# The last head pair's softmax sums on 64 rows a head, in a fused attention and convolution kernel on one NeuronCore

## The chip, the cores and the metric

The kernel runs on 1 core of one Trainium2 chip, in one launch. The metric is the device time of that launch in microseconds (us), the median of 3 runs.

## The reference

Two residual layers are applied to `x` of shape (8, 768, 32, 32), all in float32. Each normalises its input over 32 groups of channels first (`_gn`).

```
x = x + _L0_conv_ref(_gn(x), W_qkv, W_proj, b_proj)    # layer 0
x = x + _L1_conv_ref(_gn(x), conv_w, conv_b)           # layer 1

# layer 0, per image: 1024 tokens, 12 heads of 64 channels
q, k, v = (x_flat @ W_qkv.T) split in three
var_v, var_k = variance of v and of k over the 64 channels of a head (ddof=1)
attn = softmax(var_v @ var_k^T * 64**-0.5)             # 1024 x 1024 a head, of rank 1 before the softmax
out  = (attn @ v) @ W_proj.T + b_proj

# layer 1: a 1x1 convolution over the 768 channels and 28 correlations of the
# normalised feature with itself, shifted along four lines through a 7x7 window
out = einsum('bchw,oc->bohw', concat([feature, corr]), conv_w) + conv_b
```

`q` is not used. What matters here is `attn @ v`, its division by the softmax's sums, and the projection that reads the result.

## The kernel before

The work goes image by image (0 to 7). For each image there are, in the order of TensorE's program: products for keys and values (`KeysValues`), attention of the 12 heads as six pairs `hp` = 0 to 5 (`Pair`, `Attention`), and the projection (`project`). The convolution of the image before (`Conv`) and the second half of the keys' and values' products are strewn among the attention steps to keep TensorE busy. The big products follow a scheme of seven products for a 2 x 2 block; a product is named by its group and its number, (g, p), and `LOWS` gives the projection's order: (0,1), (2,1), (1,1), (0,5), (1,5), (2,5), then (0,6), (1,6) and so on, and at the end (2,6), (2,3), (2,7), (2,2), (2,4).

**The order of instructions.** Each engine runs its instructions in the order in which the Python program issues them; semaphores between engines are added automatically. That order is made by a planner, the class `Clock`: `clock.now` is a planned time, `pass_time(us)` moves it on after a unit of TensorE's work was issued, and `later.after(us, job)` has a job issue its instructions when the planned time reaches it. `clock.dve` is the planned end of VectorE's queue, and `after_dve(us, job)` counts from there. A planned time only decides what is issued before what; on the chip an instruction waits for its data.

**Evictions.** `Banks` hands out PSUM banks to the products. `Banks.close` plans the eviction of a product (a VectorE addition) for 0.1 us after the product's planned end, which is just after the next product was issued. In `project` group 2 uses the two banks of a tile `own`, the bank pair of attention's results, as its "home" slots.

**A pair.** For each of 8 blocks of keys, ScalarE computes the exponentials `ex` (L764) and TensorE multiplies them with the values into `av` (L789). The softmax's sums come in one of two ways. For some pairs ScalarE computes exponentials a second time with the accumulated sum (`denominators`, L774), and `invert` and `spread` invert and transpose the sums and write them to DRAM. For the pairs in `SUMMED` (0, 3, 4, 5 in image 0, and 3, 4, 5 in the others) VectorE adds up the exponentials in two tiles `acc`, one for each head, and a product with ones sums over the partitions. For all pairs but the last, `load_inverses` then loads the inverses from DRAM into `rd` and sets `rd_at`, the planned time of their arrival; `try_finish` plans `finish`, the multiply `v<-v,rd` on VectorE, for then. `rdpool` has one buffer, so a pair's load is issued only after the pair before has finished.

**The last pair** (`hp` = 5) ends in `sum_up_last`. Four matmuls with 32 columns of ones (`ones_products`, L820) put the sums of two heads and two halves of the tokens on four groups of 32 partitions of one bank `den`. Two reciprocals write the inverses to `acc[1]`, and eight DMAs of 64 KB (L886), four on SP's queue and four on ACT's, copy them to the 64 partitions of each head in `acc[0]`. The multiply then is `v<-v,acc`.

**The projection.** `project` issues `t1o` (`TokenSums.first`) and the first six products, which need pairs 0 to 2 alone. Before the seventh it waits, in planned time, for the last pair; `TokenSums.second` (tiles `t2o`) is issued ahead of the first product (from the third on) that is issued after the last pair's multiply. The seventh product (0,6) is the first to read `t2o`.

## Time and profile before

| | |
|---|---|
| median of 3 runs | 2656.31 us (2655.44 to 2657.39) |
| profiled execution | 2660.47 us, span 2658.7 us |
| TensorE matmul (PE) busy | 2605.5 us, 98% |
| VectorE (DVE) busy | 1576.7 us, 59% |
| ScalarE (ACT) busy | 1367.2 us, 51% |
| GpSimd (POOL) busy | 414.9 us, 16% |
| DMA | 452.39 MB, mean 170 GB/s |
| mean granted TensorE clock | 0.994 |

A view's row names the line of the kernel, the engine, the operation and the tiles it writes and reads (`out<-in`); a timeline's row begins with its start and its length in us, merges like instructions (`x12`), and ends with the idle time before it and what ended that. A float32 matmul shows as two records, so a product of six matmuls shows as `x12`. L347 is the helper that issues products, L164 the wrapper of all VectorE instructions, so tiles tell them apart. SPq is SP's queue, which issues most DMAs in order.

### The profile page before, as it was taken

The numbers are of one execution on the slowest core, as the hardware profiler recorded it, in microseconds if no ns is written. First come the engines' busy times: TensorE is split into PE (matmuls) and PEld (weight loads), VectorE is DVE, ScalarE is ACT, GpSimd is POOL, SyncE is SP. The second block draws the span as 40 slices with busy tenths as digits, with TensorE's granted clock in tenths as the row PEclk, the third lists the DMA queues.
The fourth block names the chain that finished last, engine by engine and source line by source line (L and its number), as shares of the span: only waits on it lengthen the run. The fifth ranks groups of instructions, "written<-read, shape, count | busy, mean of one in ns | idle before, by whom it ended". The sixth has DMA issues, their size and how long they took to land.

```text
span 2658.7 us, 40713 instructions
## 1 busy us (share of the span) xinstructions
PE 2605.5 (98%) x14814; PEld 1361.2 (51%) x14814; DVE 1576.7 (59%) x4094; ACT 1367.2 (51%) x1841; POOL 414.9 (16%) x444
## 2 busy tenths in 40 slices
PE   9999999999999999999999989999999999999999
PEld 5654455334764247642476424764247643575333
DVE  5868634865348653486535765357753576535764
ACT  1497089701797017970189601896018960189500
POOL 4320130003300043000430003300033001320000
PEclk9999999999999999999999999999999999999999
DMA  7875467365563645636556355563554646545333
GB/s 284 293 243 170 131 196 208 96 201 159 174 200 102 209 151 170 198 113 199 157 169 197 124 184 154 171 207 115 190 169 154 200 126 197 165 137 168 120 98 104
DMA packets 326926, 452.39 MB, mean 170 GB/s; under 512 B 60738, under 2 KB 246450, under 8 KB 326726
## 3 DMA queue, kind: packets, MB, share of 16 engines
q1 hardware_dynamic: 323958, 444.93, 52.9%
q10 hardware_dynamic: 2768, 4.85, 0.5%
q8 instruction: 118, 1.93, 0.3%
q14 instruction: 82, 0.67, 0.1%
HBM read 376.70 MB, written 64.40 MB: 166 GB/s over the span
## 4 chain that ended last, share of the span: by engine, by line
PE 92%; DVE 3%; DMA 3%; SPq 1%; issue 1%; ACT 0%; POOL 0%; DVEq 0%; ACTq 0%; POOLq 0%
PE x L347 33%; PE av L789 24%; PE y L347 16%; PE z L347 9%; PE own L347 4%; PE gr L1131 3%; DMA acc<-acc 1%; PE den L820 1%; DMA wt<-tsp 1%; DVE xn L164 1%; DVE f L164 1%; PE y L1038 1%; DVE acc L164 0%; PE z L1038 0%; SPq L886 0%
## 5 line engine op out<-in xcount | busy, mean ns | idle before, releaser
L764 ACT ACTIVATE ex<-bc,nk 128x1024 f32<-128x1024 f32 x768 | 826.8, 1137 | 409.3 <-DMA bc<-vdr 172.7
L789 PE MATMUL av<-ex,v 128*64 128x512 f32 x3072 | 697.5, 594 | 2.7 <-ACT ex L764 2.6
L789 PEld LDWEIGHTS av<-ex,v 128*64 128x64 f32 x3072 | 333.2, 137 | 318.1 <-issue 182.7
L774 ACT ACTIVATE junk<-bk,vm 128x1024 bf16<-128x1024 f32 x368 | 420.5, 1143 | 27.7 <-DMA bk<-kdr 18.0
L164 DVE TENSOR_TENSOR acc<-acc,ex 128x1024 f32<-128x1024 f32 x300 | 345.1, 1212 | 0.0
L226 ACT COPY kp<-x 128x384 f32<-128x384 f32 x28 | 13.4, 478 | 572.5 <-PE x L347 563.8
L347 PE MATMUL y<-kv,s 128*64 128x384 f32 x1488 | 267.6, 487 | 0.0
L347 PE MATMUL x<-kv,xn 128*64 128x384 f32 x1512 | 262.6, 486 | 1.1 <-issue 1.1
L347 PE MATMUL x<-kv,s 128*64 128x384 f32 x1488 | 256.7, 486 | 0.0
L347 PEld LDWEIGHTS x<-kv,xn 128*64 128x64 f32 x1512 | 143.1, 137 | 100.0 <-issue 83.9
L347 PEld LDWEIGHTS x<-kv,s 128*64 128x64 f32 x1488 | 144.3, 137 | 91.5 <-issue 72.3
L347 PEld LDWEIGHTS y<-kv,s 128*64 128x64 f32 x1488 | 140.9, 137 | 89.8 <-issue 74.0
L520 POOL TENSOR_TENSOR rstda<-vea,neghalf 128x1 f32<-128x1 f32 x8 | 4.8, 597 | 1005.1 <-DVE vea L164 1005.1
L1116 POOL TENSOR_TENSOR turn<-f,ones 128x384 f32<-128x384 f32 x112 | 111.0, 1012 | 241.1 <-PE gr L1131 154.6
L347 PE MATMUL z<-kv,xn 128*64 128x384 f32 x768 | 134.7, 486 | 0.0
L347 PE MATMUL x<-f,wt 128*64 128x512 f32 x504 | 119.0, 593 | 0.0
L626 POOL TENSOR_TENSOR s<-xn 128x384 f32<-128x384 f32 x64 | 67.7, 1068 | 311.3 <-PE x L347 190.7
L164 DVE TENSOR_TENSOR v<-y,v 128x128 f32<-128x128 f32 x180 | 41.0, 282 | 125.7 <-PE y L347 125.7
L164 DVE TENSOR_TENSOR v<-v,rd 128x1024 f32<-128x1024 f32 x40 | 48.7, 1218 | 101.4 <-DMA rd<-di 79.8
L164 DVE BATCH_NORM_STATS2 vbn<-v 128x6 f32<-128x64 f32 x720 | 101.6, 210 | 0.0
L347 PEld LDWEIGHTS z<-kv,xn 128*64 128x64 f32 x768 | 76.7, 137 | 45.9 <-issue 37.3
L1131 PEld LDWEIGHTS gr<-f,turn 128*64 128x64 f32 x1344 | 89.4, 136 | 11.3 <-issue 1.5
(200 smaller groups left out, 3093.0 us busy)
## 6 DMA issues: line engine op xcount, KB each, us to landing
kv<-kvs SPq DMA_DIRECT2D x124, 576.0 KB
kv<-in_wkv_dram SPq DMA_DIRECT2D x95, 576.0 KB
bc<-vdr SPq DMA_DIRECT2D x96, 512.0 KB
f<-in_x_dram SPq DMA_DIRECT2D x48, 512.0 KB
bk<-kdr SPq DMA_DIRECT2D x46, 512.0 KB
x1d<-f SPq DMA_DIRECT2D x42, 512.0 KB
xn<-x1d SPq DMA_DIRECT2D x42, 512.0 KB
out_dram<-xn SPq DMA_DIRECT2D x82, 256.0 KB
```

The source lines that it names most:

```text
L164: return getattr(self.engine, name)(*args, **kw)
L226: nc.scalar.copy(to, at)
L347: nc.tensor.matmul(out[at], lhsT=lhsT[:, at], rhs=rhs, start=start, stop=stop, **kw)
L520: nc.gpsimd.tensor_tensor(self.rstd, ve, neghalf[:, 0:1], ALU.pow)
L626: nc.gpsimd.tensor_tensor(self.sums[g][:, 0], a[g][2], a[g][3], ALU.add)
L764: nc.scalar.activation(ex, self.bc[e], AF.Exp, scale=self.kv.nk[self.half][:, h, t : t + 1])
L774: nc.scalar.activation(junk, self.bk[e], AF.Exp, scale=self.kv.m2[self.half][:, h, t : t + 1], accum_out=self.sums[:, e, t : t + 1],)
L789: nc.tensor.matmul(self.av[e * HD : (e + 1) * HD, hf, :], lhsT=self.vt[:, t, e, :], rhs=exs[e][:, hf * HF : (hf + 1) * HF], start=t == 0, ...
L820: nc.tensor.matmul(den[at * 32 : (at + 1) * 32, :], lhsT=ones[:, 0:32], rhs=self.acc[e][:, hf * HF : (hf + 1) * HF], start=True, stop=True,)
L1038: nc.tensor.matmul(t, lhsT=wcorr_sb[at, i, :], rhs=cs[at, tokens, :], start=False, stop=True, skip_group_check=True)
L1116: nc.gpsimd.tensor_tensor(to[:, :, side], half, windows(ones, ones.ap[0], (0, J), (HW, 4), (1, HW)), ALU.mult)
L1131: nc.tensor.matmul(ps[side * HD : (side + 1) * HD, :n].rearrange("p (y x) -> p y x", x=WIDE), lhsT=block[:, j, side, :], rhs=image[:, 4 * ...
```

## The change

1. `Banks.close`: evictions from the home slots (the two `own` banks) are planned 0.2 us earlier, so 0.1 us before the planned end of their product instead of 0.1 us after it.
2. `denominators`: in image 1, pair 2, the inversion is planned 3.0 instead of 0.5 us after the last sums.
3. `load_inverses`: for pairs 0 to 2 of every image, `rd_at` is 14 us after the load's issue; before, this held for pair 2 of image 1 alone, and all others had 8 us.
4. `sum_up_last`: four matmuls with 64 columns of ones put the sums of each head on its 64 partitions, in two banks, one for each half of the tokens. Four reciprocals of 128 x 256 write the inverses straight to `acc[0]`. The DMAs are gone. In images 1 to 7 the first reciprocal is planned 1.2 us after the products, and each other one 1.5 us after VectorE's planned queue has ended; in image 0 without these gaps.

```
         def close(self, slot, t, us, taken):
             job = self.due[slot] = lambda: taken(t)
-            clock.after(us + 0.1, lambda: self.due.get(slot) is job and self.finish(slot))
+            early = 0.2 if slot[0] == "home" else 0.0
+            clock.after(us + 0.1 - early, lambda: self.due.get(slot) is job and self.finish(slot))
...
                 self.bk_free = True
-                later.after(max(0.0, clock.act - clock.now) + 0.5, self.invert)
+                more = 3.0 if (self.b, self.hp) == (1, 2) else 0.5
+                later.after(max(0.0, clock.act - clock.now) + more, self.invert)
...
-            self.rd_at = clock.now + (14.0 if (self.b, self.hp) == (1, HP // 2 - 1) else 8.0)
+            self.rd_at = clock.now + (14.0 if self.hp < HP // 2 else 8.0)
             self.try_finish()
 
         def sum_up_last(self):
 
-            den = other([P, HF], f"den{self.b}_{self.hp}")
-            self.ones_products(den)
-            self.rd, rc = self.acc[0], self.acc[1][:, 0:HF]
-            q = HF // 2
+            dens = []
+            for hf in range(2):
+                at = slice(hf * HF, (hf + 1) * HF)
+                den = other([P, HF], f"den{self.b}_{self.hp}_{hf}")
+                for e in range(2):
+                    nc.tensor.matmul(
+                        den[e * HD : (e + 1) * HD, :], lhsT=ones, rhs=self.acc[e][:, at], start=True, stop=True
+                    )
+                dens.append(den)
+            self.rd = self.acc[0]
 
             def invert(n):
-                vector.reciprocal(rc[:, n * q : (n + 1) * q], den[:, n * q : (n + 1) * q])
-                later.after_dve(0.5, spread if n else lambda: invert(1))
-
-            def spread():
-                for at in range(4):
-                    e, hf = divmod(at, 2)
-                    to = self.rd[e * HD : (e + 1) * HD, hf * HF : (hf + 1) * HF]
-                    rows = rc[at * 32 : (at + 1) * 32, :]
-                    for half in range(2):
-                        (nc.scalar if e else nc.sync).dma_start(out=to[half * 32 : (half + 1) * 32, :], in_=rows)
-                self.rd_at = clock.now + 5.0
-                self.try_finish()
-
-            later.after(1.7 if self.b else 1.0, lambda: invert(0))
+                q = HF // 2
+                vector.reciprocal(self.rd[:, n * q : (n + 1) * q], dens[n // 2][:, n % 2 * q : (n % 2 + 1) * q])
+                if n < 3:
+                    later.after_dve(1.5 if self.b else 0.0, lambda: invert(n + 1))
+                else:
+                    self.rd_at = clock.dve
+                    self.try_finish()
+
+            later.after(1.2 if self.b else 0.0, lambda: invert(0))
```

## The prediction

> **What bounds the kernel now.** I read the page first, then the chain, then TensorE's waits, then the timelines around each wait. The page's busy times and its chain:

> ```profile
> PE 2605.5 (98%) x14814; PEld 1361.2 (51%) x14814; DVE 1576.7 (59%) x4094; ACT 1367.2 (51%) x1841; POOL 414.9 (16%) x444
> ...
> PE 92%; DVE 3%; DMA 3%; SPq 1%; issue 1%; ACT 0%; POOL 0%; DVEq 0%; ACTq 0%; POOLq 0%
> ```

> TensorE is never short of work for long, so a change counts only as far as it alters TensorE's work or its waits. TensorE's waits (total us, times, longest):

> ```profile
> PE x L347 <- DVE t2o L164: 18.9, 6, 4.8
> PE own L347 <- DVE f L164: 15.6, 14, 1.7
> PE x L347 <- DVE xn L164: 4.8, 1, 4.8
> ...
> PE av L789 <- ACT ex L764: 2.6, 2, 1.3
> ```

> The first and third are the place of `sum_up_last`: once per image, in images 1 to 7. The second is the `own` banks at the end of `project`. Timelines of image 2, TensorE, VectorE, SP queue:

> ```profile
> 874.15 1.07 PE L820 MATMUL den<-acc,ones 128*32 128x512 f32 x8
> ...
> 888.08 2.74 PE L347 MATMUL own<-t1o,wt 128*64 128x512 f32 x12
> 894.56 7.93 PE L347 MATMUL x<-t2o,wt 128*64 128x512 f32 x24 [3.74 <-DVE t2o L164]
> ```

> ```profile
> 876.24 1.75 DVE L164 RECIPROCAL acc<-den 128x256 f32<-128x256 f32 x1
> ...
> 879.76 1.75 DVE L164 RECIPROCAL acc<-den 128x256 f32<-128x256 f32 x1
> ...
> 892.68 1.23 DVE L164 TENSOR_TENSOR v<-v,acc 128x1024 f32<-128x1024 f32 x1 [3.63 <-DMA acc<-acc]
> 893.82 1.89 DVE L164 TENSOR_TENSOR t2o<-v,t1o 128x512 f32<-128x512 f32 x3
> 895.62 0.74 DVE L164 SCALAR_TENSOR_TENSOR f<-own,bproj_sb,f 128x512 f32<-128x512 f32 x1
> ```

> ```profile
> 880.56 5.67 SPq L334 DMA_DIRECT2D wt<-tsp  x3
> ...
> 887.16 2.49 SPq L886 DMA_DIRECT2D acc<-acc  x4
> ```

> The inverses are ready at 881.5, but SP's four copies stand behind weight loads that wait for TensorE to free their buffers, and go out at 887.16. The multiply (892.68), `t2o` and the seventh product follow from that. And the stall costs more than its 3.74 us: 24 matmuls last 5.15 elsewhere and 7.93 here, each at half the pace for the first product. The same half pace follows all six stalls of 3.02 to 4.82 us (images 1 to 6) and none of those up to 1.71.

> The end of `project` in image 2:

> ```profile
> 925.74 2.74 PE L347 MATMUL own<-v,wt 128*64 128x512 f32 x12
> 929.34 2.79 PE L347 MATMUL own<-v,wt 128*64 128x512 f32 x12 [0.86 <-DVE f L164]
> 931.96 2.75 PE L347 MATMUL z<-v,wt 128*64 128x512 f32 x12
> 936.41 2.80 PE L347 MATMUL own<-t4o,wt 128*64 128x512 f32 x12 [1.71 <-DVE f L164]
> ```

> ```profile
> 928.53 0.75 DVE L164 SCALAR_TENSOR_TENSOR f<-own,bproj_sb,f 128x512 f32<-128x512 f32 x1 [3.01 <-PE own L347]
> ```

> The eviction at 928.53 belongs to product (2,6), over at 925.9, but ends its wait only with (2,3), which writes the other bank: the two banks are one tile, and the kernel orders work on it as one.

> **The change, part by part.** Times are against the profiled execution (2660.47 us, span 2658.7 and 1.8 around it); it lies 4.2 above the median of the runs, 2656.31, and I carry the difference over to the median. About 0.2% (5.3 us) can be told from no change.

> *Sums on 64 rows.* Four matmuls of 32 columns take 1.00 (874.15 to the next product, 875.15); four of 64 columns are an attention step, 1.72 (6.87 per 32 records, four steps). So TensorE has 0.72 more per image. Sixteen more reciprocals of 1.75 are 28 us of VectorE, in project, where it waits for products anyway. Gone are 64 DMAs of 64 KB, with 2.5 us of issue on each of SP and ACT per image; nothing on ACT waits there.

> *The new order, images 2 to 6.* The planner's clock gives it (it counts 1.74 a reciprocal, 0.68 an eviction, 2.58 a product). With the product (0,1) issued at 0, the others follow every 2.58, the sum is issued at −1.70, the reciprocals at −0.50, 3.04, 8.86 and 12.10, the multiply at 15.33, and with the 0.2 us of `early` the eviction of (2,5) at 15.38. `t2o` comes with the seventh product, (0,6), at 15.48. Before, that eviction stood at 15.58, behind `t2o` (895.62 against 893.82). VectorE's queue is then: reciprocal, t1o, two evictions, (0,1), reciprocal, (2,1), (1,1), reciprocal, (0,5), reciprocal, (1,5), multiply, (2,5), t2o. With row durations the fourth reciprocal ends 14.7 after the sums' start, (1,5) has been evicted at 15.5 and the multiply is over at 16.7, before (2,5) ends at 17.35: the inverses no longer hold anything. But `t2o` now stands behind the eviction of (2,5): (2,5) starts at 1.72 + 5 × 2.575 = 14.6, ends 2.75 later, then 0.05, eviction 0.66, and 0.74 from t2o's start to the product: 18.8. Unheld it would be 17.2, so 1.6 of idle remains, less than any stall that halved the pace. Before, the same distance was 20.41, 20.05, 21.43, 20.34 and 19.69: 101.9 − 94.0 = 7.9 gained. The half pace after it (two products took 7.77, 6.90, 8.20, 6.90, 6.90 against 5.15) gives 10.9. Together **−18.8**.

> *Image 1.* The sum is issued 11 us ahead of project, so all four reciprocals and the multiply fit: the multiply starts at 550.7 instead of 552.31 and, what matters, no longer stands before the last evictions of the convolution. Product (1,1), which waited for these until 556.66 (gap 4.82), starts at 552.4: −4.3, and −2.6 of half pace (5.17 for a product of 2.58). **−6.9**.

> *Image 7.* The same 18.8 against 17.01 now (gap 0.34, full pace): **+1.8**.

> *Image 0.* Here VectorE also has the statistics of the next image's keys, and the planner puts the multiply at 289.90, after the copy of the value rows, the eviction of (2,5) and six small scalings. (2,5) ends at 291.45; then copy 0.25 (with its transpose 0.3), eviction 0.66, scalings 0.9, multiply 1.14, 0.74: the seventh product at 295.5 instead of 290.57. +5.0, and since 4 us of idle is more than the 3.02 that halved the pace, 1.75 to 3.05 more (I take 2.2): **+7.2**.

> *Evictions of `own` ahead of the next product.* Now (2,3) must wait for (2,6)'s eviction and (2,7) for (2,3)'s. One such turn costs 929.34 − 925.74 − 2.58 = 1.0 to 1.2 (319.16 to 322.92 in image 0: 1.18); in place of one turn per image and, in images 2 to 6, 1.87 before (2,4) (0.4 in image 1) there are two turns and nothing before (2,4), whose eviction has (2,2) to hide in. Before 8 × 1.18 + 5 × 1.87 + 0.4 = 19.2, after 16 × 1.18 = 18.9: **−0.3**. If each also finds VectorE in a 0.76 us scaling of the next image, +9; if the other bank did not count, −19.

> *The inversion of pair 2 of image 1, 2.5 us later.* VectorE waited 8.34 for it at 465.18, ahead of accumulations that free exponentials; TensorE's gap there is 1.25. I take **−1.2** (bounds 0 and −1.5).

> *Multiplies of pairs 0 to 2, 6 us later.* VectorE idles 79.8 us before 15 of them, up to 11.4, yet TensorE's waits in attention are the two of 1.3 above: cover enough, so 0. If the 23 moved multiplies of 1.22 each met an eviction on the path, +28; the row with 11.4 and no gap is the nearest.

> Sum: −18.8 − 6.9 + 1.8 + 7.2 − 0.3 − 1.2 = −18.2, so **2638**.

> [...]

> **The rivals.**

> *Nothing holds t2o* (the eviction is issued after it, or image 0's chain is shorter): 1.6 less in images 2 to 7 and 7 less in image 0: 2638 − 9.6 − 7.2 = 2621. For it: image 0 shows no stall now. Against: the 0.1 us between 15.38 and 15.48. 15%.

> *The multiply slips* (the slower side). Its place is the seventh product of images 2 to 7: planned at 15.33, with 0.15 to spare. If a shift in attention makes it later than 15.48, or a reciprocal waits, the multiply runs behind (2,5)'s eviction: 1.14 more, 2.7 idle, and the pace halves again in six images. At 2.2 each that is +20, 2658; at two windows of half pace (3.4 each, as image 4 nearly shows with 3.05) +27, and 1.2 more in image 0: 2666. Slower from 2.8 us of half pace on. 15%, half of it beyond 2661.6.

> *Image 0's stall keeps the pace*: 2636. Against: all six stalls over 3 us lost it. [...] 5%.

> *The later due times do nothing*, as their multiplies still meet their DMA: that is the term 0, the time stays 2638.

> **How the numbers follow.** Forecast 60%, its own range 2630 to 2648 by the bounds of the half pace, the own banks and pair 2; 2621 15%, 2636 5%, the slip 15%, and 5% for a reordered attention anywhere up to 2670. The range 2619 to 2659 leaves out the far half of the slip and the tails. Faster by over 0.2% (under 2651): 0.60 + 0.15 + 0.05 + 0.02 = 0.82. Slower: 0.07 + 0.02 = 0.09. The same: 0.09.

> **What would show it.** Right: no wait on `DMA acc<-acc`; in images 2 to 7 an eviction of `own` just before `t2o`, gaps near 1.4 to 1.6 before the first product of `t2o` and 5.15 for the next two; four reciprocals per image between the evictions; in image 0 a gap near 4 before the same product; two gaps of 0.86 in `own`, before (2,3) and (2,7), none before (2,4). Wrong: the multiply behind that eviction, half pace in images 2 to 7, or new gaps inside attention.

## The result and the profile after

The changed kernel takes 2645.19 us (median of 6 runs, 2642.72 to 2650.47), the kernel before 2656.43 in the same series (6 runs, 2654.74 to 2659.37). The ratio is 0.9958, with a 95% interval of 0.9946 to 0.9971: faster by 0.4%. Forecast were 2638 us and a range of 2619 to 2659.

The two profiled executions lie further apart than the medians: 2660.47 before, 4.0 above its median, and 2642.72 after, 2.5 under its own. So the traces differ by 17.75 us and the medians by 11.2. The terms below are read from the traces and sum to the first. Two executions that took 4268.76 us (`e5_image0_copied`) and 14237.98 us (the kernel before) are left out of the figures below.

The page after, busy times and chain:

```profile
PE 2598.2 (98%) x14814; PEld 1329.4 (50%) x14814; DVE 1608.2 (61%) x4110; ACT 1367.7 (52%) x1841; POOL 416.9 (16%) x444
...
PE 95%; DVE 2%; DMA 1%; ACT 0%; issue 0%; SPq 0%; POOL 0%; DVEq 0%; POOLq 0%; ACTq 0%
```

VectorE is busy 31.5 us longer (1576.7 before; sixteen more reciprocals), yet its share of the chain falls from 3% to 2%. That of DMA falls from 3% to 1%. TensorE's waits after:

```profile
PE own L347 <- DVE f L164: 14.9, 16, 2.6
PE x L347 <- DVE t2o L164: 13.1, 7, 3.6
PE av L791 <- ACT ex L765: 2.2, 2, 1.3
PE den L822 <- DVE acc L164: 2.0, 1, 2.0
```

The seventh product still waits for `t2o`, now in seven images: 3.6 in image 0 and 1.45 to 1.81 in images 2 to 7. A new wait of 2.0 before the sums of a pair (`den`) has come. Image 2 after, TensorE and then VectorE:

```profile
876.52 1.94 PE L878 MATMUL den<-acc,ones 128*64 128x512 f32 x8
...
891.16 2.75 PE L347 MATMUL own<-t1o,wt 128*64 128x512 f32 x12
895.37 5.37 PE L347 MATMUL x<-t2o,wt 128*64 128x512 f32 x24 [1.46 <-DVE t2o L164]
```

```profile
877.67 1.76 DVE L164 RECIPROCAL acc<-den 128x256 f32<-128x256 f32 x1 [0.22 <-PE den L878]
...
883.01 1.75 DVE L164 RECIPROCAL acc<-den 128x256 f32<-128x256 f32 x1
...
886.90 1.75 DVE L164 RECIPROCAL acc<-den 128x256 f32<-128x256 f32 x1
...
889.47 1.75 DVE L164 RECIPROCAL acc<-den 128x256 f32<-128x256 f32 x1
...
892.05 1.21 DVE L164 TENSOR_TENSOR v<-v,acc 128x1024 f32<-128x1024 f32 x1
893.97 0.75 DVE L164 SCALAR_TENSOR_TENSOR f<-own,bproj_sb,f 128x512 f32<-128x512 f32 x1 [0.71 <-PE own L347]
894.64 1.88 DVE L164 TENSOR_TENSOR t2o<-v,t1o 128x512 f32<-128x512 f32 x3
```

The multiply waits for nothing any more and is over at 893.26. VectorE then idles 0.71 us for the product (2,5), because the eviction at 893.97 has been issued ahead of `t2o`. The next two products take 5.37 and not 7.93: the half pace is gone.

### The profile page after: what moved, and what is told of

It is laid out like the page before. It is cut to its first block, busy times and chain, and to the rows that moved or that the text cites. A ratio compares the mean times of both kernels' runs of the same rounds, so it can differ in the third digit from the quotient of the medians.

```text
span 2641.0 us, 40631 instructions
## 1 busy us (share of the span) xinstructions
PE 2598.2 (98%) x14814; PEld 1329.4 (50%) x14814; DVE 1608.2 (61%) x4110; ACT 1367.7 (52%) x1841; POOL 416.9 (16%) x444
## 3 DMA queue, kind: packets, MB, share of 16 engines
q10 hardware_dynamic: 1232, 2.75, 0.3%
## 4 chain that ended last, share of the span: by engine, by line
PE 95%; DVE 2%; DMA 1%; ACT 0%; issue 0%; SPq 0%; POOL 0%; DVEq 0%; POOLq 0%; ACTq 0%
PE x L347 34%; PE av L791 25%; PE y L347 17%; PE z L347 9%; PE own L347 5%; PE gr L1134 3%; DVE f L164 1%; PE den L822 1%; PE den L878 1%; PE y L1041 1%; PE z L1041 1%; DMA f<-in_x_dram 0%; ACT ex L765 0%; DMA bc<-vdr 0%; DMA xn<-in_x_dram 0%
## 5 line engine op out<-in xcount | busy, mean ns | idle before, releaser
L791 PEld LDWEIGHTS av<-ex,v 128*64 128x64 f32 x3072 | 324.6, 137 | 329.9 <-issue 206.6
L164 DVE TENSOR_TENSOR acc<-acc,ex 128x1024 f32<-128x1024 f32 x300 | 345.1, 1212 | 0.0
L347 PE MATMUL y<-kv,s 128*64 128x384 f32 x1488 | 266.8, 487 | 0.0
L347 PE MATMUL x<-kv,xn 128*64 128x384 f32 x1512 | 262.3, 486 | 1.1 <-issue 1.1
L347 PE MATMUL x<-kv,s 128*64 128x384 f32 x1488 | 256.6, 486 | 0.0
L347 PEld LDWEIGHTS x<-kv,xn 128*64 128x64 f32 x1512 | 137.9, 137 | 106.9 <-issue 91.2
L347 PEld LDWEIGHTS x<-kv,s 128*64 128x64 f32 x1488 | 140.1, 137 | 95.9 <-issue 80.0
L347 PEld LDWEIGHTS y<-kv,s 128*64 128x64 f32 x1488 | 134.2, 137 | 93.2 <-issue 80.5
L347 PE MATMUL z<-kv,xn 128*64 128x384 f32 x768 | 135.1, 486 | 0.0
L164 DVE TENSOR_TENSOR v<-y,v 128x128 f32<-128x128 f32 x180 | 40.9, 282 | 126.4 <-PE y L347 126.3
L347 PE MATMUL x<-f,wt 128*64 128x512 f32 x504 | 117.8, 592 | 0.0
L164 DVE BATCH_NORM_STATS2 vbn<-v 128x6 f32<-128x64 f32 x720 | 101.6, 209 | 0.0
L347 PEld LDWEIGHTS z<-kv,xn 128*64 128x64 f32 x768 | 73.8, 137 | 48.8 <-issue 40.6
L164 DVE SCALAR_TENSOR_TENSOR xn<-x,bconv_sb,xn 128x512 f32<-128x512 f32 x63 | 46.4, 745 | 80.8 <-PE x L347 79.7
```

The costliest lines, as they stand in the source:

```text
L164: return getattr(self.engine, name)(*args, **kw)
L347: nc.tensor.matmul(out[at], lhsT=lhsT[:, at], rhs=rhs, start=start, stop=stop, **kw)
L791: nc.tensor.matmul(self.av[e * HD : (e + 1) * HD, hf, :], lhsT=self.vt[:, t, e, :], rhs=exs[e][:, hf * HF : (hf + 1) * HF], start=t == 0, ...
```

## The experiments

All were timed against the kernel before on the same chip; its median lay between 2658.3 and 2660.2 in these series.

**The parts alone.** `e1_no_early` is the change without its first edit:

```
-            early = 0.2 if slot[0] == "home" else 0.0
-            clock.after(us + 0.1 - early, lambda: self.due.get(slot) is job and self.finish(slot))
+            clock.after(us + 0.1, lambda: self.due.get(slot) is job and self.finish(slot))
```

> The changed kernel with the home slots' evictions planned 0.1 us after their product again; the rest of the change stays. Theory: in images 2 to 7 what still holds t2o is the eviction of (2,5), which the earlier plan puts in front of it; without it t2o comes 1.6 us earlier, the gaps of 1.45 to 1.81 before the seventh product go under 0.3, and the projection's end costs about what it did (0.1 less). Time: 2645.2 - 9.7 = 2635.5, ratio 0.992 to the kernel before. Rival: it is the multiply, behind four reciprocals, that is late; then the gaps stay and the time is 2645.

Measured: 2633.79 us (2632.58 to 2634.86), ratio 0.9908 (0.9894 to 0.9921). Image 2 in this kernel, VectorE and TensorE:

```profile
887.76 1.22 DVE L164 TENSOR_TENSOR v<-v,acc 128x1024 f32<-128x1024 f32 x1
888.90 1.89 DVE L164 TENSOR_TENSOR t2o<-v,t1o 128x512 f32<-128x512 f32 x3
890.70 0.74 DVE L164 SCALAR_TENSOR_TENSOR f<-own,bproj_sb,f 128x512 f32<-128x512 f32 x1
```

```profile
889.63 5.37 PE L347 MATMUL x<-t2o,wt 128*64 128x512 f32 x24
```

`t2o` stands ahead of the eviction, and the seventh product waits for nothing. So the earlier eviction is what still holds `t2o` in the change, in images 2 to 7. It costs some 11 us by the medians and 10.1 by the spans of the two traces, and at the end of `project` it gains 0.3.

`e2_sums_only` is the kernel before with the fourth edit alone, the new `sum_up_last`:

```
-            den = other([P, HF], f"den{self.b}_{self.hp}")
-            self.ones_products(den)
...
+                    nc.tensor.matmul(
+                        den[e * HD : (e + 1) * HD, :], lhsT=ones, rhs=self.acc[e][:, at], start=True, stop=True
+                    )
...
```

> The kernel before with the new sums of the last pair alone (no earlier evictions, no later due times). Theory: these sums carry the whole gain. Against the run without the earlier evictions alone, image 0 does not get its gap of 2.04 before the sums of pair 4 (1.9 less), and image 1 gets back its gap of 1.25 in attention (1.2 more): 2635 to 2636, ratio 0.992. Rival: the later due times free VectorE (it waited 79.8 us for the inverses' DMA before) and TensorE gains from it; then this kernel is 5 us or more slower than with them.

Measured: 2634.40 us (2632.90 to 2635.58), 0.9908 (0.9893 to 0.9924). The sums alone gain 24 us, more than the whole change's 11. Image 0's stall is there too:

```profile
295.06 8.37 PE L347 MATMUL x<-t2o,wt 128*64 128x512 f32 x24 [3.61 <-DVE t2o L164]
```

It is as long as in the change, 3.61, but here half pace follows (8.37 against 5.37).

`e3_later_only` is the kernel before with the second and third edits, the later due times:

```
-                later.after(max(0.0, clock.act - clock.now) + 0.5, self.invert)
+                more = 3.0 if (self.b, self.hp) == (1, 2) else 0.5
+                later.after(max(0.0, clock.act - clock.now) + more, self.invert)
...
-            self.rd_at = clock.now + (14.0 if (self.b, self.hp) == (1, HP // 2 - 1) else 8.0)
+            self.rd_at = clock.now + (14.0 if self.hp < HP // 2 else 8.0)
```

> The kernel before with the later due times alone: the multiplies of pairs 0 to 2 planned 14 us after their load, and the inversion of pair 2 of image 1 2.5 us later. Theory: TensorE hardly waits in attention, so 0 there, 1.2 less in image 1 and 1.9 more in image 0 (gap before the sums of pair 4): 2657, ratio 1.000. Rival: VectorE's freed waits help: 2650 or less.

Measured: 2660.75 us (2655.86 to 2663.65), 1.0005 (0.9996 to 1.0014): nothing, as expected. It has the new wait of 2.04 before `den` that `e2_sums_only` lacks, so the due times make that wait. Its place in image 0, before and then after the change:

```profile
239.43 7.04 PE L789 MATMUL av<-ex,v 128*64 128x512 f32 x32
246.30 2.11 PE L347 MATMUL y<-kv,s 128*64 128x384 f32 x12
248.60 2.19 PE L820 MATMUL den<-acc,ones 128*32 128x512 f32 x8 [0.20 <-DVE acc L164]
```

```profile
239.71 2.11 PE L347 MATMUL y<-kv,s 128*64 128x384 f32 x12
241.65 7.04 PE L791 MATMUL av<-ex,v 128*64 128x512 f32 x32
250.72 3.06 PE L822 MATMUL den<-acc,ones 128*32 128x512 f32 x8 [2.04 <-DVE acc L164]
```

The moved multiply has shifted the plan, and a keys' and values' product that stood between the attention steps and the sums, where it covered the last accumulations, is now issued ahead of the steps. `e7_best` below, which leaves image 0's multiplies where they were, has 0.20 there again.

`e5_image0_copied` is `e1_no_early` with the old sums and copies, as `sum_up_copied`, in image 0:

```
-                    later.after_dve(0.5 if self.b or last else 3.0, self.sum_up_last if last else self.sum_up)
+                    later.after_dve(0.5 if self.b or last else 3.0, (self.sum_up_last if self.b else self.sum_up_copied) if last else self.sum_up)
```

> The run without the earlier evictions, with the old sums and copies of the last pair in image 0 alone. Theory: in image 0 VectorE has no room for two more reciprocals, and t2o came 3.6 us late there; with the copies the gap of 3.6 before the seventh product goes, and 0.8 of the sums' products: 4.4 less, 2629.5, ratio 0.9895; up to 3 more in runs in which that gap had halved the pace. Rival: the sums' order in image 0 isn't what is late; 2634.

Measured: 2628.77 us (2628.74 to 2629.60, three executions), 0.9886 (0.9867 to 0.9905). From the sums to the seventh product image 0 takes 20.37 again, as before, and 25.66 in the change.

**The half pace.** `e6_kept_busy` is the kernel before with products that nobody reads ahead of the stalled one:

```
+            if n == (2 if b == 1 else 6) and 0 < b < NB - 1:
+                spare = small(f"spare{b}")
+                for _ in range(12):
+                    nc.tensor.matmul(spare[:, 0:P], lhsT=ident, rhs=ident, start=True, stop=True)
```

> The kernel before with twelve spare products of 128 x 128 (nobody reads them) on TensorE ahead of the product that stalled, in images 1 to 6: the stall stays, but 2.6 us of it are filled. Theory: the half pace after the stall comes from the idle time itself, so it goes and the stall's length stays: the two products after it take 5.2 and not 6.9 to 8.2; 11 to 13 us less, 2644, ratio 0.995. Rival: the slow products wait for something else (weights or pieces of t2o arriving late): then the time is 2656 as before, or longer by the spare products that outlast the stall.

Measured: 2649.03 us (2647.49 to 2651.37), 0.9967 (0.9955 to 0.9980): 9 us instead of 11 to 13. Image 2:

```profile
887.71 2.94 PE L1431 MATMUL spare<-ident 128*128 128x128 f32 x24
893.17 7.07 PE L347 MATMUL x<-t2o,wt 128*64 128x512 f32 x24 [2.52 <-DVE t2o L164]
```

With this work in them, the gaps of images 1 to 6 were 1.3, 2.5, 0.7, 1.9, 0.3 and 0.7; only those of 2.5 and 1.9 were followed by half pace. So it is the idle time that costs the pace. Where 2.5 us stay idle, it is lost all the same.

**The accumulators of `own`.** `e4_split_banks` is `e1_no_early` with the two-bank tile as two tiles of one bank:

```
-        own = avp.tile([P, 2, HF], F32, tag="av", name=f"own{b}")
-        wide.home = {"x": own[:, 0, :], "y": own[:, 1, :]}
+        own = [avp.tile([P, HF], F32, tag=f"av{n}", name=f"own{n}_{b}") for n in range(2)]
+        wide.home = {"x": own[0], "y": own[1]}
...
```

> The run without the earlier evictions, with attention's tile of two banks made into two tiles of one bank each, for attention and for the projection's home slots. Theory: the waits of 0.86 and 1.71 at the projection's end come from the two banks being ordered as one tile; with two tiles an eviction waits for its own product alone. The end of the projection, now 18.7 us longer than its products over the eight images, shrinks to them: 2634 - 18 = 2616, ratio 0.984. Rival: the turn is VectorE's, late with work in front of the evictions; then the gaps stay, 2634.

Measured: 2616.06 us (2615.77 to 2616.14), 0.9836 (0.9822 to 0.9850). Image 2's end of `project`:

```profile
914.91 2.77 PE L347 MATMUL own<-t2o,wt 128*64 128x512 f32 x12
917.51 5.32 PE L347 MATMUL own<-v,wt 128*64 128x512 f32 x24
```

(2,6), (2,3) and (2,7) follow each other without a gap. These waits came from the two banks being one tile, and 17.7 us hung on them (2633.79 less 2616.06). The edit also splits attention's `av` and the correlations' tile, which share the two banks.

**The copies' queue.** The prediction put the stall down to the place of four copies in SP's queue. `e8_copies_on_act` has ScalarE issue all eight, in the kernel before; `e9_act_and_split` has the split banks as well:

```
-                        (nc.scalar if e else nc.sync).dma_start(out=to[half * 32 : (half + 1) * 32, :], in_=rows)
+                        nc.scalar.dma_start(out=to[half * 32 : (half + 1) * 32, :], in_=rows)
```

> The kernel before with all eight copies of the last pair's inverses issued by ACT; nothing else changes. Theory: the old stall is SP's queue, in which four copies stood behind weight loads that wait for TensorE. ACT is idle there; eight issues of 0.61 from 881.6 in image 2 end at 886.5, and 3.0 after that, as before, the multiply starts: 889.5 instead of 892.7. The gaps in images 2 to 6 fall under 1 us and the pace stays full: about 5.3 an image, 7 in image 1: 2657 - 34 = 2623, ratio 0.987. Rival: copies through DMA need their 11 us from the reciprocal to the multiply whichever queue issues them; then 2650 or more, and only the new sums could take the stall away.

> The kernel before with both: the copies on ACT and the tile of two banks split. Theory: both gains add, as they lie in different stages: 2623 - 18 = 2605, ratio 0.980; no part of the studied change is in it. Rival: without the waits at the projection's end the next image's normalisation becomes late and takes the gain back: 2615 or more.

Measured: 2672.43 us, 1.0053 (1.0040 to 1.0067), slower; and 2653.01, 0.9976 (0.9966 to 0.9987), where the split banks take their 19 us off and the stall stays (34.3 us in six waits of up to 7.9). My theory, that the place in SP's queue is the cause and ACT's queue the cure, had expected 2623. Image 2 of `e8_copies_on_act`, ACT's queue, SP's and VectorE:

```profile
876.39 8.41 ACTq L886 DMA_DIRECT2D acc<-acc  x8
```

```profile
882.74 5.46 SPq L222 DMA_DIRECT2D xn<-in_x_dram  x6
```

```profile
891.45 1.23 DVE L164 TENSOR_TENSOR v<-v,acc 128x1024 f32<-128x1024 f32 x1 [7.06 <-DMA acc<-acc]
```

The copies start early and land late. Two causes offered themselves: SP, freed, now sends the six 512 KB loads of the next image beside them, or eight copies are too many for one queue. `e10_loads_later` was to tell them apart; it is `e8_copies_on_act` with one due time in `Conv.done` moved:

```
-                later.after(9.0, self.after)
+                later.after(17.0, self.after)
```

> The kernel before with all eight copies of the inverses issued by ScalarE, and the loads of the next image (with what follows them) planned 8 us later, so that they no longer run beside the copies. Theory (the six loads of 512 KB share the DMA with the copies and make them late): the copies land some 3 us after the last issue, the multiply of image 2 starts at about 888 instead of 891.45, the gaps before the seventh product fall from 5 to 10 us to 2 to 4, and the time falls from 2672 to 2640 to 2655. Rival (eight issues of 1.05 us on one queue and the copies themselves are slow): the last copy still lands at 891 and the gaps and the time stay, 2665 to 2675. If the next image's loads then come too late for its keys, TensorE waits there for xn; such a gap is taken off first.

Measured: 2671.93 us, 1.0050 (1.0036 to 1.0064). The time is the same, but it does not settle the two causes, because the later loads made waits of their own. TensorE's waits in `e8_copies_on_act`, then in `e10_loads_later`:

```profile
PE x L347 <- DVE t2o L164: 38.7, 6, 9.8
```

```profile
PE x L347 <- DVE t2o L164: 21.5, 6, 4.5
...
PE y L347 <- POOL s L626: 8.5, 6, 1.4
```

The stall shrank by 17.2 us, so the loads were part of it. Against that stand 8.5 us of waits for `s`, a tile made from the next image's normalised input, which `e8_copies_on_act` does not have. With the loads away 21.5 us of waits for `t2o` stay, no less than the 18.9 of the kernel before. Image 2, where those loads come after the multiply:

```profile
880.45 6.96 ACTq L886 DMA_DIRECT2D acc<-acc  x8
```

```profile
892.04 1.22 DVE L164 TENSOR_TENSOR v<-v,acc 128x1024 f32<-128x1024 f32 x1 [4.40 <-DMA wt<-in_wproj_dram]
```

So `e11_copies_on_pool` is the kernel before with SP's four given to GpSimd's queue, ScalarE's four as they were:

```
-                        (nc.scalar if e else nc.sync).dma_start(out=to[half * 32 : (half + 1) * 32, :], in_=rows)
+                        (nc.scalar if e else nc.gpsimd).dma_start(out=to[half * 32 : (half + 1) * 32, :], in_=rows)
```

> The kernel before with the four copies that SP issued given to GpSimd's queue, ScalarE's four as they were: neither queue then has a weight load ahead of the copies, and neither has eight to issue. If the place in SP's queue is what makes the copies late, both queues are done with their four some 2.5 us after the second reciprocal (884.0 in image 2), the copies land 3.0 later as SP's did (multiply at 887 instead of 892.68), the seventh product waits for nothing or for under 1 us in images 2 to 6 and keeps its pace, and the time is about 2656 - 31 = 2625. Rival: the copies land late whichever queue issues them, since other transfers share the DMA: the multiply starts at 890 or later, stalls of 2.5 to 5 us stay, and the time is 2645 to 2675.

Measured: 2627.25 us (2625.47 to 2628.24), 0.9870 (0.9849 to 0.9891). Image 2, GpSimd, VectorE and TensorE:

```profile
876.30 2.19 POOL L886 DMA_DIRECT2D acc<-acc  x4 [119.56 <-DVE f L164]
```

```profile
883.19 1.21 DVE L164 TENSOR_TENSOR v<-v,acc 128x1024 f32<-128x1024 f32 x1
```

```profile
885.06 5.37 PE L347 MATMUL x<-t2o,wt 128*64 128x512 f32 x24
```

GpSimd had been idle for 119.56 us and issues at once. The multiply waits for nothing and neither does the product; only 1.85 in image 4 and 0.85 in image 6 remain, at full pace. The prediction's reading of the stall holds: SP's four copies were late by their place. `e8_copies_on_act` had replaced one late queue by another and put the next image's loads beside it. On average over images 2 to 6 the multiply starts 11.5 us after the second reciprocal in the kernel before, 14.9 in `e8_copies_on_act`, 11.1 in `e10_loads_later` and 8.3 in `e11_copies_on_pool`. By the trace's packets of image 2 the eight copies on ACT's queue ran from 879.30 to 890.48 (11.2 us; 8.8 in `e10_loads_later`), the four and four of `e11_copies_on_pool` from 878.14 to 882.13.

**The best versions.** `e7_best` is `e4_split_banks` with image 0's old copies, and without the later multiplies in image 0:

```
-            self.rd_at = clock.now + (14.0 if self.hp < HP // 2 else 8.0)
+            self.rd_at = clock.now + (14.0 if self.b and self.hp < HP // 2 else 8.0)
```

`e12_pool_and_split` is `e11_copies_on_pool` with the split banks: the old sums and none of the change's four edits.

> The change without the earlier evictions, with the accumulators of attention and of own as two one-bank tiles each, image 0's sums and copies as before, and the later multiplies only from image 1 on. If the terms found so far add up, this is the split version's 2616.1, less image 0's stall and what its VectorE work cost (2633.8 - 2629.2 = 4.6 by the version with image 0 copied), less the 1.9 that the reordered attention of image 0 cost: 2609 to 2610, ratio 0.981. Rival: the reordered product in image 0 comes from the planner's state and another gap takes its place: 2611.5. TensorE's waits should have no entry of own, of t2o or of den above 0.3 us.

> The kernel before with the four copies of SP given to GpSimd's queue (2627.3 by itself) and the accumulators of attention and of own as two one-bank tiles (17.7 by itself, 2633.8 - 2616.1): 2609.5, with no new sums, no earlier eviction and no other due times. If so, the two costs add and the new sums are one way of two to take away the first. Rival: without the waits in own the copies have less time in hand and the seventh product stalls again by 1 to 2 us in most images: 2613 to 2620.

Measured: 2608.06 us (2607.44 to 2608.28), 0.9809 (0.9795 to 0.9822), and 2606.21 us (2605.34 to 2608.20), 0.9799 (0.9780 to 0.9817). Both beat the changed kernel by about 1.5%, and their intervals overlap. The longest of TensorE's waits left in `e7_best`:

```profile
PE av L790 <- ACT ex L764: 2.2, 2, 1.3
PE gr L1156 <- DVE win L164: 2.0, 4, 1.0
```

Nothing of `own` or `t2o` is left in its list, and `den` has 0.2. In `e12_pool_and_split` two waits for `t2o` of 0.3 and 0.6 stay: its rival had 1 to 2 in most images.

## Why the prediction was right, and where its terms were off

The direction and the mechanism came out, and so did the sum of the traces: forecast −18.2, measured −17.75. Term by term, from the starts of the same products in both traces:

| term | forecast | measured |
|---|---|---|
| images 2 to 6, sums to seventh product | −7.9 | −7.0 |
| images 2 to 6, half pace after it | −10.9 | −10.65 |
| image 1 | −6.9 | −6.8 |
| image 7 | +1.8 | +1.8 |
| image 0, gap and half pace | +7.2 | +5.1 |
| end of `project` | −0.3 | −0.3 |
| pair 2 of image 1 | −1.2 | −1.15 |
| later multiplies | 0 | +1.9 |
| the rest, not forecast | | −0.65 |
| sum | −18.2 | −17.75 |

That the sums lie within 0.5 us of each other is in part luck: image 0 came out 2.1 under its term, since its pace was kept in this execution, and the later multiplies cost 1.9 where the forecast had nothing.

*Images 2 to 6.* The order of VectorE's queue is as worked out, with multiply, (2,5), `t2o` in a row. From the sums to the seventh product take 18.85 and 18.84 in images 2, 5 and 6 (forecast 18.8) and 19.19 and 19.20 in images 3 and 4. The first rival, that nothing would hold `t2o`, was the state of `e1_no_early`; the 0.1 us of planned time decided against it. The multiply did not slip either.

*Image 1.* It went as worked out: the convolution's last evictions (554.27 and 554.88) now stand ahead of the multiply (558.15), and product (1,1) starts 17.1 after the sums, as forecast, and waits for nothing.

*Image 0.* The multiply stands where forecast, behind the copy, the eviction and the scalings:

```profile
294.25 0.28 DVE L164 COPY rsv<-ptv 48x128 f32<-48x128 f32 x1 [1.87 <-PE own L347]
294.45 0.73 DVE L164 SCALAR_TENSOR_TENSOR f<-own,bproj_sb,f 128x512 f32<-128x512 f32 x1
295.11 0.88 DVE L164 TENSOR_SCALAR nk<-km,most 128x8 f32<-128x8 f32 x6
295.91 1.21 DVE L164 TENSOR_TENSOR v<-v,acc 128x1024 f32<-128x1024 f32 x1
```

The way from the sums to the seventh product is 5.3 longer, near the forecast 5.0, and the gap is 3.61, but the 2.2 of half pace did not come in this execution: the rival with 5%. The same 3.61 halved the pace in `e2_sums_only` and `e4_split_banks` and kept it in `e1_no_early`. In this execution two windows of the clock shared the gap, as the last section shows. The chance of 5%, the author's estimate, was far too small: the pace was kept in two of the four profiles with this gap.

*End of `project`.* Two gaps near 0.8 per image, before (2,3) and (2,7) and none before (2,4), as forecast:

```profile
925.00 2.79 PE L347 MATMUL own<-v,wt 128*64 128x512 f32 x12 [0.85 <-DVE f L164]
928.60 2.80 PE L347 MATMUL own<-v,wt 128*64 128x512 f32 x12 [0.80 <-DVE f L164]
```

The sum of −0.3 is luck as well: images 2 to 6 gained 0.92 each, where the forecast's terms gave 0.69 (1.87 less 1.18), and image 1 took that back. There the bad case came once: the eviction at 600.19 stood behind two scalings, and (2,3) waited 2.59.

```profile
598.75 1.52 DVE L164 TENSOR_SCALAR xn<-xn,meana,rstda 128x1024 f32<-128x1024 f32 x2
600.19 0.74 DVE L164 SCALAR_TENSOR_TENSOR f<-own,bproj_sb,f 128x512 f32<-128x512 f32 x1
```

*Later multiplies.* This is the step that failed, a term put at 0: it looked for the cost where the moved multiplies land, and found cover there. The cost came from what the plan did with the shifted time, a product that changed places with four attention steps (2.04 before `den`, and the half pace after it).

*From the trace to the median.* The difference of one trace was carried over to the median unchanged. That is the larger part of the miss, 2645 against 2638: the profiled execution before lay 4.0 above the median of the second series, the one after 2.5 under its own. Of the other five executions of the change only the time and the mean granted clock are on record. The clock was 0.999 in three, as in the profiled one, and 0.998 and 0.997 in the two slowest (2650.47 and 2647.04). That some of them halved the pace in image 0, at 1.7 to 3.0 us as in `e4_split_banks` and `e2_sums_only`, would account for most of that 2.5, but is argued, not shown.

## What to carry to other kernels

Look at the next instruction in the queue, not only at the wait that a change removes: here the wait for the copies was truly gone, and an eviction issued 0.2 us earlier held the same product in its place, at some 10 to 11 us. Copies that stand behind waiting transfers may need another queue and not other work in their place, as long as they aren't all piled on one: four moved to an idle queue gave 1.3%, all eight on one lost 0.5%. A wait on an accumulator that was evicted long ago is worth a look at whether it shares a tile with one that was not; making two tiles of it gave 17.7 us.

## What the runs showed of the hardware

```profile
248.16:251.57 3.41, 1.37 (x8) 1.00 0.50 132
251.57:254.98 3.41, 3.40 (x10) 0.50 0.40 91
292.53:295.94 3.41, 1.64 (x8) 1.00 0.29 85
295.94:299.36 3.42, 1.58 (x8) 1.00 0.13 39
```

**Copies on one queue and on two.** In image 2, eight copies of 64 KB on one queue, among other transfers, took 8.8 us (`e10_loads_later`), and 11.2 with the next image's loads beside them (`e8_copies_on_act`). Four on each of two queues took 4.0 (`e11_copies_on_pool`), and ACT's four in the kernel before 3.7. So a queue took 1.1 to 1.4 us a copy where it had eight and 0.9 to 1.0 where it had four, and in `e11_copies_on_pool` two queues did so side by side. The issue on ACT's queue shrank from 8.41 to 2.45 us from `e8_copies_on_act` to `e11_copies_on_pool`, yet the last packets also came nearer to the last issue, 3.7 us after it against 5.7: between these two runs more was gained than the issue. Why is open. GpSimd's copies also differ in form: the profile of `e11_copies_on_pool` lists them as `software_dynamic`, in 64 packets of 4 KB, and ACT's four as `hardware_dynamic`, in 128 of 2 KB.
